# A reordered first normalisation, and casts bound behind a gelu, in a fused time-mix and GELU feed-forward kernel

## The chip, the cores and the metric

The kernel runs on one core of a Trainium2 chip. The metric is device time in microseconds (us) for one execution. A core has five engines with a queue each: TensorE (PE, with its weight loads PEld), VectorE (DVE), ScalarE (ACT), GpSimd (POOL) and SyncE (SP), which here issues all transfers between HBM and the on-chip memory. An engine works through its queue in order; semaphores tie the engines together.

## The reference

The input `x` has 4 sequences of 1024 tokens with 512 channels in float32. It is normalised per token to `xn`, and two branches are added to it.

```python
xn = _layernorm(x, axis=-1)
# branch 1, time mix: token t is mixed with token t-1 (token 0 with token 1)
xx = jnp.concatenate([xn[:, 1:2, :], xn[:, :-1, :]], axis=1) - xn
k = jnp.einsum('btc,hc->bth', xn + xx * time_mix_k, Wk)      # 704 hidden channels
r = jnp.einsum('btc,hc->bth', xn + xx * time_mix_r, Wr)
w = jnp.exp(-jnp.exp(time_decay))
state = state * w + jax.nn.relu(k_t)                        # a scan over t
out = layernorm(einsum(state * r_t, Wv)) * gamma + beta
# branch 2, feed-forward: 2048 hidden channels
X = xn.astype(jnp.float16)
D = jax.nn.gelu(jnp.dot(X.astype(jnp.float32), W0.T) + bias0, approximate=False).astype(jnp.float16)
E = jnp.dot(D.astype(jnp.float32), W1.T) + bias1
return x + out + E.astype(jnp.float16)
```

## The kernel before

The tokens are cut into 8 blocks of 512 (`blocks`), two for each sequence; a block has four tiles `s` of 128 tokens, and the 512 channels are four chunks `c` of 128. W0 and W1 are held as two parts, a rounded high part and the low rest (`split`, L123: ScalarE casts the high part, L124, VectorE subtracts it for the low part, L125), so that each product with them is made twice.

Each block goes through the same stages on TensorE:

- `attention` (L361): for each of six groups of hidden channels the products pk and pr (L385) from the mixed inputs `xk` and `xnT`; ScalarE takes the relu (L370), VectorE scans (L372) and multiplies by pr (L396).
- `ffn` (L470): `up(n)` (L475) makes the n-th of 16 hidden chunks, pd (L480), ScalarE takes its gelu to fp16 (L488), VectorE casts it to the product's type, d (L490). `down(n, s)` (L493) multiplies d with w1 and adds up pe (L495). Step n of the loop (L508) issues `up(n + 2)` and then the four `down(n, s)`. So a product up(n) has two further steps until down(n) wants its d.
- Between steps other work is issued, by the table `between` (L550): at step 0 `attention_out` (L413), at step 4 the next block's normalisation (`layernorm`, L189), at step 7 the next block's transposition on VectorE (`transposed`, L198, sixteen transposes at L204) and its mixing (`mixed_inputs`, L331). The mixing, for each chunk c, casts the normalised input to fp16 on ScalarE (L343), takes the difference to the token before (L348) and makes xk and then xnT from it (L350). xnT is overwritten in place, so its write has to wait for the cast that reads it.

Outside two stretches with an order written out by hand the framework's scheduler places the instructions in each engine's queue; the place at which work is issued in the program is its guide, not the final order.

Block 0 has extra work: W0 is loaded and split during `attention` (`load_w0`, L133), and W1 is loaded, split and written back to HBM in the split form during `ffn` (`load_w1`, L140; raw tiles from a ring of three, w1 tiles from another ring of three). Later blocks only read the split form back.

The first block's input has nothing to hide behind. `first_inputs` (L209) therefore has an order of its own under `manual_schedule` (L261 to L315). For each tile s: `stats` (L233) takes mean and variance on VectorE, `deviations` (L236) the square roots of two tiles on ScalarE, `inverses` (L241) their reciprocals on VectorE. `normalized` (L244) scales the tile: tile 0 on ScalarE with a shift computed on VectorE (L247, L248), the others on VectorE (L187). `turned` (L252) transposes the tile's four chunks on TensorE into `pts`. `busy(n)` (L228) issues n products of the identity with itself, whose result nobody reads; each appears as two instructions in the profile. Four edge transposes (L275) give the first two tokens, and a small one turns the mix rows (L284). Then ScalarE and VectorE build xk and xnT from the transposed chunks (L310, L313), and the first pk product can start. The fp16 casts of block 0 (L322) come after that.

Of the kernel before, what the change touches and what calls it, by code (L numbers as in the profile page):

```python
# [9 lines left out]
F32 = mybir.dt.float32  # L10
F32R = mybir.dt.float32r
AF = mybir.ActivationFunctionType
ALU = mybir.AluOpType

P = 128
# [4 lines left out]
def time_mix_and_gelu_ffn(  # L20
# [26 lines left out]
    nc = tc.nc  # L47
# [5 lines left out]
    NC = C // P  # L53
# [16 lines left out]
    const = pool("const", 1)  # L70
# [17 lines left out]
    ident = const.tile([P, P], F32, name="ident")  # L88
# [5 lines left out]
    eps_sb = const.tile([P, 1], F32, name="eps_sb")  # L94
    nc.vector.memset(eps_sb, EPS)
    mix_rows = const.tile([2 * NC, P], F32, name="mix_rows")
# [5 lines left out]
    b0_sb = const.tile([P, NN], F32, name="b0_sb")  # L102
# [106 lines left out]
    def first_inputs(xs, behind):  # L209

        pts = [ps_e.tile([P, TB], F32, tag="pe", name=f"pt_0_{c}") for c in range(NC)]
        idle = ps_mm.tile([P, TB], F32, tag="mm", name="idle")
        small = ps_mm.tile([P, TB], F32, tag="mm", name="small")
        tail = ps_mm.tile([P, TB], F32, tag="mm", name="tail")
        mix_t = small[:, : 2 * NC]
        late_t = tail[:, : NF + 1 + NN]
        edge = ps_mm.tile([P, TB], F32, tag="mm", name="edge")  # L220
        edge_t = edge[:, : NC * 2].rearrange("p (c t) -> p c t", t=2)
        mv = two.tile([P, NS, 2], F32, tag="mv", name="mvx_0")
        rstd = two.tile([P, NS], F32, tag=f"rstd{NS}", name="rx_0")
        shift0 = const.tile([P, 1], F32, name="shift0")
        ends = const.tile([P, NC, 2], F32, name="ends")
        xk = one.tile([P, NC, TB], F32, tag="xk", name="xk_0")

        def busy(n):  # L228

            for _ in range(n):  # L230
                nc.tensor.matmul(idle[:, :P], ident, ident, start=True, stop=True)

        def stats(s):  # L233
            stats_of(mv, s, xs[:, s, :], f"stx_0_{s}")

        def deviations(s0):  # L236
            nc.scalar.activation(
                rstd[:, s0 : s0 + 2], mv[:, s0 : s0 + 2, 1], AF.Sqrt, bias=eps_sb
            )

        def inverses(s0):  # L241
            nc.vector.reciprocal(rstd[:, s0 : s0 + 2], rstd[:, s0 : s0 + 2])

        def normalized(s):  # L244
            x_s, r = xs[:, s, :], rstd[:, s : s + 1]
            if s == 0:
                nc.vector.scalar_tensor_tensor(shift0, mv[:, 0, 0:1], -1.0, r, ALU.mult, ALU.mult)  # L247
                nc.scalar.activation(x_s, x_s, AF.Identity, bias=shift0, scale=r)  # L248
            else:
                normalize(x_s, x_s, mv[:, s, 0:1], r)  # L250

        def turned(s):  # L252
            for c in range(NC):
                nc.tensor.transpose(
                    pts[c][:, s * P : (s + 1) * P], xs[:, s, c * P : (c + 1) * P], ident
                )

        steps = [(0, 0), (1, 0), (0, 1), (1, 1), (2, 0), (3, 0), (2, 1), (3, 1)]  # L260
        with tc.manual_schedule(  # L261
            engines={nc.scalar.engine, nc.vector.engine, nc.tensor.engine}
        ):

            nc.scalar.activation(shift0, eps_sb, AF.Sqrt)
            busy(13)
            stats(0)
            stats(1)
            deviations(0)
            stats(2)  # L270
            inverses(0)
            normalized(0)
            turned(0)
            for c in range(NC):
                nc.tensor.transpose(  # L275
                    edge_t[:, c, :], xs[:2, 0, c * P : (c + 1) * P], ident[:2, :2]
                )
            busy(1)
            stats(3)
            deviations(2)  # L280
            normalized(1)
            nc.scalar.copy(ends, edge_t)
            turned(1)
            nc.tensor.transpose(mix_t, mix_rows, ident[: 2 * NC, : 2 * NC])  # L284
            nc.scalar.copy(mix_sb, mix_t)
            nc.scalar.activation(rest_sb, mix_t, AF.Identity, bias=1.0, scale=-1.0)
            inverses(2)
            normalized(2)
            turned(2)
            normalized(3)  # L290
            turned(3)
            nc.tensor.transpose(
                late_t, late_rows, ident[: NF + 1 + NN, : NF + 1 + NN]
            )
            busy(5)

            apart = two.tile([P, NC], F32, tag="apart", name="apart")
            nc.vector.tensor_sub(apart, ends[:, :, 1], ends[:, :, 0])
            for dst, m in ((xk[:, :, 0], mk_sb), (xnT[:, :, 1], mr_sb)):
                part = two.tile([P, NC], F32, tag="part", name="part")  # L300
                nc.vector.tensor_mul(part, apart, m)
                nc.vector.tensor_add(dst, part, ends[:, :, 0])
            for c, kind in steps:
                if kind == 0:
                    dst = part = xk[:, c, 1:]
                else:
                    ar = two.tile([P, TB], F32, tag="xx", name=f"ar_0_{c}")
                    dst, part = xnT[:, c, 2:], ar[:, 1:]
                j = kind * NC + c
                scaled = nc.scalar.activation(  # L310
                    part, pts[c][:, 1:], AF.Identity, scale=rest_sb[:, j : j + 1]
                )
                mixed = nc.vector.scalar_tensor_tensor(  # L313
                    dst, pts[c][:, : TB - 1], mix_sb[:, j : j + 1], part, ALU.mult, ALU.add
                )  # L315

        behind.enter_context(tc.issue_after(scaled.ins))
        behind.enter_context(tc.issue_after(mixed.ins))
        x16s = []
        for c, pt in enumerate(pts):  # L320
            x16 = four.tile([P, TB], F16, tag="x16", name=f"x16_0_{c}")
            nc.scalar.copy(x16, pt)  # L322
            x16s.append(x16)
            nc.scalar.copy(last[:, c, :], pt[:, TB - 1 :])

        nc.scalar.activation(w_sb, late_t[:, : NF + 1], AF.Exp)
        nc.scalar.activation(w_sb, w_sb, AF.Exp, scale=-1.0)
        nc.scalar.copy(b0_sb, late_t[:, NF + 1 :])
        return x16s, xk

    def mixed_inputs(i):  # L331

        t0 = blocks[i][1]
        if t0 > 0:
            nc.gpsimd.tensor_copy(xnT[:, :, 0:1], last)
        x16s = []
        xk = one.tile([P, NC, TB], F32, tag="xk", name=f"xk_{i}")
        for c in range(NC):
            now = xnT[:, c, 1:]
            if t0 == 0:  # L340
                nc.vector.tensor_copy(xnT[:, c, 0:1], now[:, 1:2])
            x16 = four.tile([P, TB], F16, tag="x16", name=f"x16_{i}_{c}")
            nc.scalar.copy(x16, now)  # L343
            x16s.append(x16)
            if t0 + TB < T:
                nc.gpsimd.tensor_copy(last[:, c, :], xnT[:, c, TB : TB + 1])
            xx = two.tile([P, TB], F32, tag="xx", name=f"xx_{i}_{c}")
            nc.vector.tensor_sub(xx, xnT[:, c, :TB], now)  # L348
            for dst, m in ((xk[:, c, :], mk_sb), (now, mr_sb)):
                nc.vector.scalar_tensor_tensor(  # L350
                    dst, xx, m[:, c : c + 1], now, ALU.mult, ALU.add
                )
        return x16s, xk
# [116 lines left out]
    def ffn(i, xf, between, state):  # L470
# [4 lines left out]
        def up(n):  # L475
            pd = ps_mm.tile([P, TB], F32, tag="mm", name=f"pd_{i}_{n}")
            cols = slice(n * P, (n + 1) * P)
            for c in range(NC):
                for w in (w0h, w0l):
                    nc.tensor.matmul(  # L480
                        pd,
                        w[c][:, cols],
                        xf[:, c, :],
                        start=(c == 0 and w is w0h),
                        stop=(c == NC - 1 and w is w0l),
                    )
            d16 = two.tile([P, TB], F16, tag="d16", name=f"d16_{i}_{n}")
            nc.scalar.activation(d16, pd, AF.Gelu, bias=b0_sb[:, n : n + 1])  # L488
            d = wide.tile([P, TB], F32R, tag="d", name=f"d_{i}_{n}", bufs=4)
            nc.vector.tensor_copy(d, d16)  # L490
            return d
# [36 lines left out]
    for i in range(len(blocks)):  # L528
# [16 lines left out]

        def next_inputs():
            transposed(x_now)
            state["mixed"] = mixed_inputs(i + 1)

        between = {0: out_stage}  # L550
        if more:
            between[4] = next_norm
            between[7] = next_inputs
        pe = ffn(i, xf, between, state)
        if more:
            x16s, xk = state["mixed"]
# [46 lines left out]
```

## Time and profile before

| | |
|---|---|
| Median of 4 runs | 944.82 us (944.48 to 945.03) |
| The profiled execution, its own time | 944.65 us |
| Its span, first to last instruction | 942.7 us |
| Start of the first pk product | 11.74 us |
| Busy share of TensorE / VectorE / ScalarE | 99% / 52% / 17% |
| Block 0, from its first pk to that of block 1 | 117.26 us |
| Blocks 1 to 6, each | 115.52 us |
| From the last block's first pk to the end | 120.41 us |

The profile is of one execution. A line of a timeline gives the start, the duration (of a whole run of instructions where they are merged), the engine, the line of the kernel, the operation, output and inputs, and in square brackets how long the engine sat idle before it and what ended that. A line of the waits gives who waited for whom, in total, how often, and the longest. The chain of waits follows the last instruction back to what released it, step by step; its dates cut the blocks above. Matmul ends are modelled, so neighbouring matmuls overlap in the listing; their starts are the better measure.

### The profile page before, as it was taken

To read this page: it belongs to the slowest core of one execution; us is meant where nothing else is said; L and a number is where in the kernel's file an instruction comes from. 1 tells how busy PE (TensorE), PEld (TensorE's weight loads), DVE (VectorE), ACT (ScalarE), POOL (GpSimd) and SP (SyncE) were. 2 spreads that over 40 slices of the span, in tenths; PEclk is the share of its full clock that TensorE was granted. 3 is DMA by queue.
4 is the path that set the end of the run, shared out by engine and by line. 5 is a ranking of instruction groups with operands and counts; after the bars stand their busy time and mean duration, and the time that the engine had idled before them with its cause. 6 is when DMAs were issued, how large, how long until landed. Compare 5 with 4: busy or idle time off the path is not lost.

```text
span 942.7 us, 8746 instructions
## 1 busy us (share of the span) xinstructions
PE 935.1 (99%) x3260; PEld 588.0 (62%) x3260; DVE 486.1 (52%) x842; ACT 162.7 (17%) x265; POOL 51.8 (5%) x124
## 2 busy tenths in 40 slices
PE   9999999999999999999999999999999999999998
PEld 6447764478544885448854588445884458744686
DVE  6558752484425944359343592426923279332513
ACT  6323410012100220102201021010210102111021
POOL 0010000100001000011000100002000020000100
PEclk9999999999999999999999999999999999999999
DMA  8734660035400454014530154302542023510243
GB/s 293 238 131 152 226 232 0 23 134 189 146 1 26 141 192 133 1 33 158 189 111 1 39 182 164 107 0 68 183 161 80 0 89 135 170 54 1 71 152 112
DMA packets 39573, 106.49 MB, mean 113 GB/s; under 512 B 4431, under 2 KB 4460, under 8 KB 39532
## 3 DMA queue, kind: packets, MB, share of 16 engines
q1 hardware_dynamic: 39532, 105.94, 33.3%
q8 instruction: 26, 0.43, 0.2%
q14 instruction: 15, 0.12, 0.0%
HBM read 89.14 MB, written 16.78 MB: 112 GB/s over the span
## 4 chain that ended last, share of the span: by engine, by line
PE 94%; DVE 4%; issue 1%; DMA 0%; ACT 0%; POOL 0%; SPq 0%; DVEq 0%
PE pd L480 23%; PE pe L495 22%; PE po L420 15%; PE pr L385 15%; PE pk L385 15%; PE pkr L385 3%; PE po L430 2%; DVE xnT L204 1%; DVE w L125 0%; DMA x<-in_L_attn_x 0%; DVE stx L183 0%; DVE d L490 0%; DVE z L467 0%; DVE e L466 0%; DVE xk L350 0%
## 5 line engine op out<-in xcount | busy, mean ns | idle before, releaser
L495 PE MATMUL pe<-w,d 128*128 128x512 f32 x1024 | 251.0, 389 | 1.4 <-DVE w L125 0.8
L495 PEld LDWEIGHTS pe<-w,d 128*128 128x128 f32 x1024 | 192.0, 188 | 42.3 <-DVE d L490 1.5
L480 PE MATMUL pd<-xf,w0h 128*128 128x512 f32 x512 | 203.5, 397 | 0.0
L480 PE MATMUL pd<-xf,w0l 128*128 128x512 f32 x512 | 199.4, 389 | 0.0
L488 ACT ACTIVATE d<-pd,b_sb 128x512 f16<-128x512 f32 x128 | 87.9, 687 | 418.8 <-PE pd L480 408.5
L385 PE MATMUL pr<-xnT,wr 128*128 128x512 f32 x320 | 144.2, 591 | 0.0
L385 PE MATMUL pk<-xk,wk 128*128 128x512 f32 x320 | 144.1, 592 | 0.0
L420 PE MATMUL po<-wv_sb,g 128*128 128x512 f32 x320 | 140.8, 595 | 0.0
L490 DVE CAST d<-d 128x512 fp32r<-128x512 f16 x128 | 54.0, 424 | 130.3 <-ACT d L488 129.3
L480 PEld LDWEIGHTS pd<-xf,w0h 128*128 128x128 f32 x512 | 96.1, 188 | 28.1 <-issue 5.7
L480 PEld LDWEIGHTS pd<-xf,w0l 128*128 128x128 f32 x512 | 96.1, 188 | 21.4 <-issue 1.9
L385 PEld LDWEIGHTS pr<-xnT,wr 128*128 128x128 f32 x320 | 60.5, 189 | 76.9 <-issue 75.7
L420 PEld LDWEIGHTS po<-wv_sb,g 128*128 128x128 f32 x320 | 60.1, 190 | 75.7 <-issue 75.0
L385 PEld LDWEIGHTS pk<-xk,wk 128*128 128x128 f32 x320 | 60.6, 190 | 73.4 <-issue 72.0
L204 DVE STREAM_TRANSPOSE xnT<-x 32x512 f32<-32x512 f32 x112 | 78.7, 703 | 2.2
L372 DVE TENSOR_TENSOR_SCAN st<-w_sb,carry,rk 128x512 f32<-128x512 f32 (+1 forms) x24 | 30.8, 1283 | 70.3 <-ACT rk L370 70.3
L370 ACT ACTIVATE rk<-pk 128x512 f32<-128x512 f32 x40 | 23.9, 597 | 233.6 <-PE pk L385 233.6
L183 DVE BATCH_NORM_STATS2 sty<-po 128x6 f32<-128x512 f32 x32 | 22.1, 689 | 73.5 <-PE po L430 67.9
L372 DVE TENSOR_TENSOR_SCAN st<-w_sb,rk 128x512 f32<-128x512 f32 (+1 forms) x24 | 29.3, 1222 | 55.3 <-ACT rk L370 53.5
L396 DVE TENSOR_TENSOR g<-st,pr 128x512 f32<-128x512 f32 x40 | 27.5, 687 | 53.6 <-PE pr L385 53.6
L177 POOL TENSOR_SCALAR ry<-mvy 128x1 f32<-128x1 f32 x32 | 11.4, 357 | 502.5 <-DVE mvy L184 502.5
L466 DVE TENSOR_TENSOR e<-pe,b_sb 128x512 f16<-128x512 f32 x32 | 20.8, 685 | 17.0 <-PE pe L495 17.0
(75 smaller groups left out, 458.7 us busy)
## 6 DMA issues: line engine op xcount, KB each, us to landing
w<-w1d SPq DMA_DIRECT2D x111, 512.0 KB, 3.2
x<-in_L_attn_x SPq DMA_DIRECT2D x32, 256.0 KB, 3.3
xres<-in_L_attn_x SPq DMA_DIRECT2D x32, 256.0 KB, 2.7
w1d<-w SPq DMA_DIRECT2D x16, 512.0 KB, 2.9
out<-z SPq DMA_DIRECT2D x32, 256.0 KB, 5.1
w0raw<-in_L_ffn_W SPq DMA_DIRECT2D x16, 256.0 KB, 4.9
w1raw<-in_L_ffn_W SPq DMA_DIRECT2D x16, 256.0 KB, 3.4
wk<-in_L_attn_Wk SPq DMA_DIRECT2D x4, 352.0 KB, 4.3
```

The source lines that it names most:

```text
L183: nc.vector.bn_stats(st6, src)
L204: nc.vector.transpose(dst[i * Q : (i + 1) * Q, :, :, j, :], src[j * Q : (j + 1) * Q, :, :, i, :],)
L370: nc.scalar.activation(rk[:hw], pk, AF.Relu)
L372: nc.vector.tensor_tensor_scan(st[:hw], w_sb[:hw, h : h + 1].to_broadcast([hw, TB]), rk[:hw], 0.0 if t0 == 0 else carry[:hw, h : h + 1], A ...
L385: nc.tensor.matmul(dst, w[c][:, cols], src, start=(c == 0), stop=(c == NC - 1))
L396: nc.vector.tensor_mul(g[:, h, :], st, pr)
L420: nc.tensor.matmul(pos[s], g[:, h, s * P : (s + 1) * P], wv_sb[:, h, :], start=(first and h == 0), stop=(not first and h == NF - 1),)
L466: nc.vector.tensor_add(e16, pe, b1_sb)
L480: nc.tensor.matmul(pd, w[c][:, cols], xf[:, c, :], start=(c == 0 and w is w0h), stop=(c == NC - 1 and w is w0l),)
L488: nc.scalar.activation(d16, pd, AF.Gelu, bias=b0_sb[:, n : n + 1])
L490: nc.vector.tensor_copy(d, d16)
L495: nc.tensor.matmul(pe[s], d[:, s * P : (s + 1) * P], w1[part], start=(n == 0 and part == 0), stop=(n == NN - 1 and part == 1),)
```

## The change

In the first block's order:

- tile 1 is normalised on ScalarE too, with a shift of its own (`shifts` has two columns);
- tile 2's statistics come after the reciprocals, shifts and scalings of tiles 0 and 1, directly ahead of tile 3's;
- on TensorE, the identity products at the start go from 13 to 11 calls, the one call between the edge transposes and tile 1 goes, and two calls stand behind the small transpose of the mix rows, ahead of tile 2. `turned(1)` and the small transpose are written before tile 3's statistics.

In the steady part:

- `mixed_inputs` takes the latest gelu that has been issued, and its four casts to fp16 are issued under `issue_after` that gelu, which holds them behind it in the scheduler's order;
- in block 0 the next block's transposition and mixing are issued at step 9 of the feed-forward loop instead of 7. The latest gelu is then that of up(10); in the other blocks it is that of up(8).

```diff
-        shift0 = const.tile([P, 1], F32, name="shift0")
+        shifts = const.tile([P, 2], F32, name="shifts")
...
-            if s == 0:
-                nc.vector.scalar_tensor_tensor(shift0, mv[:, 0, 0:1], -1.0, r, ALU.mult, ALU.mult)
-                nc.scalar.activation(x_s, x_s, AF.Identity, bias=shift0, scale=r)
+            if s < 2:
+                shift = shifts[:, s : s + 1]
+                nc.vector.scalar_tensor_tensor(
+                    shift, mv[:, s, 0:1], -1.0, r, ALU.mult, ALU.mult
+                )
+                nc.scalar.activation(x_s, x_s, AF.Identity, bias=shift, scale=r)
...
-            nc.scalar.activation(shift0, eps_sb, AF.Sqrt)
-            busy(13)
+            nc.scalar.activation(shifts[:, :1], eps_sb, AF.Sqrt)
+            busy(11)
             stats(0)
             stats(1)
             deviations(0)
-            stats(2)
             inverses(0)
             normalized(0)
+            normalized(1)
             turned(0)
             for c in range(NC):
                 nc.tensor.transpose(
                     edge_t[:, c, :], xs[:2, 0, c * P : (c + 1) * P], ident[:2, :2]
                 )
-            busy(1)
+            turned(1)
+            nc.tensor.transpose(mix_t, mix_rows, ident[: 2 * NC, : 2 * NC])
+            busy(2)
+            stats(2)
             stats(3)
             deviations(2)
-            normalized(1)
             nc.scalar.copy(ends, edge_t)
-            turned(1)
-            nc.tensor.transpose(mix_t, mix_rows, ident[: 2 * NC, : 2 * NC])
             nc.scalar.copy(mix_sb, mix_t)
...
-    def mixed_inputs(i):
+    def mixed_inputs(i, behind):
...
-            nc.scalar.copy(x16, now)
+            with tc.issue_after(behind.ins):
+                nc.scalar.copy(x16, now)
...
-            nc.scalar.activation(d16, pd, AF.Gelu, bias=b0_sb[:, n : n + 1])
+            state["gelu"] = nc.scalar.activation(d16, pd, AF.Gelu, bias=b0_sb[:, n : n + 1])
...
-            state["mixed"] = mixed_inputs(i + 1)
+            state["mixed"] = mixed_inputs(i + 1, state["gelu"])
...
-            between[7] = next_inputs
+            between[9 if i == 0 else 7] = next_inputs
```

## What I expect of the change

> **What bounds the kernel now.** I read the page's busy time by engine first (PE 99% of the span, DVE 52%), then the busy time by block, then TensorE's waits, then the timelines around the only gaps that these show. The blocks are cut at the first pk product of each (L385), as the chain of waits dates them.
>
> ```profile
> 11.91:129.17 117.26, 116.19 (x401) 72.39 (x401) 81.56 (x139) 44.09 (x77) 7.65 (x17) 1.00 0.61 212
> 129.17:244.69 115.52, 115.52 (x402) 72.41 (x401) 60.03 (x106) 16.55 (x26) 7.17 (x15) 1.00 0.31 103
> 244.69:360.21 115.52, 115.52 (x402) 72.41 (x401) 59.41 (x102) 16.55 (x26) 6.08 (x16) 1.00 0.30 101
> ```
>
> The columns are the stretch, its length, then busy time and count of PE, PEld, DVE, ACT and POOL. Blocks 1 to 6 are each 115.52 us long and TensorE is busy for all of it: nothing off TensorE can shorten them. Block 0 is 1.74 us longer. Before it lie 11.91 us in which the first block is normalised. So the change has two places in which to win: 1.74 us in block 0, and part of 11.91 us.
>
> TensorE's waits name the first place, and its timeline sizes it:
>
> ```profile
> PE pe L495 <- DVE w L125: 0.8, 1, 0.8
> PE pe L495 <- DVE d L490: 0.6, 2, 0.3
> ...
> 107.17 0.39 PE L480 MATMUL pd<-xf,w0l 128*128 128x512 f32 x1
> 107.87 0.50 PE L495 MATMUL pe<-w,d 128*128 128x512 f32 x1 [0.31 <-DVE d L490]
> 109.13 1.89 PE L495 MATMUL pe<-w,d 128*128 128x512 f32 x7 [0.76 <-DVE w L125]
> 110.86 0.39 PE L480 MATMUL pd<-xf,w0h 128*128 128x512 f32 x1
> ```
>
> Products follow each other every 0.227 us, so without a wait down(9) starts at 107.40 and the next up(12) 1.81 later, at 109.21. It starts at 110.86: 1.65 us lost. The rest of the 1.74 is 0.08 in the first pk products (11.91 to 13.71 where later fours take 1.72).
>
> Why VectorE is late there:
>
> ```profile
> 99.39 1.66 ACT L343 CAST x<-xnT 128x512 f16<-128x512 f32 x3 [3.87 <-DVE xnT L204]
> 100.96 0.68 ACT L488 ACTIVATE d<-pd,b_sb 128x512 f16<-128x512 f32 x1
> ...
> 107.39 0.42 DVE L490 CAST d<-d 128x512 fp32r<-128x512 f16 x1
> 107.72 0.75 DVE L350 SCALAR_TENSOR_TENSOR xnT<-xx,mix_sb,xnT 128x512 f32<-128x512 f32 x1
> 108.38 0.69 DVE L125 TENSOR_TENSOR w<-w1raw,w 128x512 fp32r<-128x512 f32 x1
> ```
>
> ScalarE stands 3.87 us before the casts of the next block's input, which wait for VectorE's transposes; gelu 8 is queued behind them, though its product ended at 96.52. VectorE then does the mixing for block 1 (L348, L350, 102.2 to 107.4) before d 9 and the low half of w1 9, which TensorE needs at 107.40. The mixing itself is not needed until 129.17.
>
> The second place, the opening:
>
> ```profile
> 5.35 0.69 DVE L183 BATCH_NORM_STATS2 stx<-x 128x6 f32<-128x512 f32 x1
> 5.44 0.29 ACT L237 ACTIVATE rx<-mvx,eps_sb 128x2 f32<-128x2 f32 x1 [3.23 <-DVE mvx L184]
> ...
> 6.17 0.13 DVE L242 RECIPROCAL rx<-rx 128x2 f32<-128x2 f32 x1
> 6.34 0.16 DVE L247 SCALAR_TENSOR_TENSOR shift<-mvx,rx 128x1 f32<-128x1 f32 x1
> ...
> 6.54 0.81 ACT L248 ACTIVATE x<-x,shift,rx 128x512 f32<-128x512 f32 x1 [0.80 <-DVE shift L247]
> ...
> 7.40 0.66 PE L254 MATMUL pt<-ident,x 128*128 128x128 f32 x4 [0.62 <-ACT x L248]
> ```
>
> The square root is done at 5.73, but the reciprocal waits behind the third tile's statistics until 6.17. From 7.40 on TensorE runs without a gap until the first product.
>
> **What the Trainium skill says.** "Perfetto Trace Analysis", Identifying the Most-Contended Engine, warns that matmul busy time overstates how close TensorE is to its limit. For blocks 1 to 6 the trace supports the bound otherwise: six equal lengths. "ScalarE: Activation LUTs", What ACT_TABLE_LOAD costs, gives 280 ns + 0.833 ns per element with a pointer bias, about 93 ns more for a pointer scale, and 93 ns of overlap between neighbours: an estimate of 0.80 us for a 512-wide tile, where the trace has 0.81; the second tile then follows 0.72 after the first. "TensorE: Matmul & The Clock Gate", What's actually happening, says that TensorE starts at half clock and needs a busy window of about 3.4 us. The trace agrees in kind: the idle products on the identity are 0.21 us apart until about 6.1 us and about 0.11 after it (the granted clock reads 1.00 throughout).
>
> **Opening, part by part.** The reciprocal moves ahead of the third tile's statistics. It can start at 5.73 + 0.04 = 5.77; the first shift follows 0.17 later (5.94), ScalarE 0.20 after that (6.14), and the first tile is normalised at 6.95: 0.40 us earlier, so the first transposes start at 7.00. The second shift is hidden beside ScalarE. The second tile goes to ScalarE at 6.14 + 0.72 = 6.86 and is done at 7.67; VectorE loses the 0.52 us operation for it. TensorE wants it after four transposes and the four edge transposes, at 7.00 + 0.93 = 7.93: covered by 0.26.
>
> What is late next is the rest of VectorE. Third statistics at about 6.10, fourth at 6.92 (before 6.42), its mean at 7.64; root on ScalarE at 7.86; reciprocal 8.18; third and fourth tiles at 8.39 and 8.87, done 8.91 and 9.41, 0.5 later than before. TensorE reaches the third at 9.06 to 9.26 and the fourth at 9.50 to 9.70: the cover is 0.1 to 0.2 us, and beyond it each delay counts in full.
>
> TensorE's own queue: the single idle call (two instructions) between edge and second tile goes, but two calls (four instructions) stand after the small transpose. Two more at 0.11 is 0.22 us to pay against 0.40 won. With each gap even at 0.11 the first transpose of the fourth tile, which starts ScalarE's first mix, comes at 9.55 against 9.83 (gain 0.28). With the 0.165 to 0.21 us that the trace shows behind an edge or small transpose, it comes at 9.61 to 9.70 (gain 0.13 to 0.22). Bounds: nothing, if the fourth tile is late; the whole 0.40 if the idle work costs nothing. I take 0.23. The eleven starting idle calls (two fewer, four instructions at 0.21) only follow the earlier transposes; the four small VectorE operations end at about 10.1, before the first mix at 10.7, so they stay hidden. The copy of the mix rows waits for nothing new. Everything behind (mix, idle, pk) is a fixed sequence and moves by the same 0.23. The weights' transfers are not moved in this stage.
>
> **Block 0.** The mixing moves from step 7 to step 9 and its casts are bound behind the latest gelu, number 10. As built, ScalarE does gelu 8, split 9, gelu 9, split 10, gelu 10, then the four casts. VectorE does the first two differences and xk products, d 8, then w 9, d 9, w 10, d 10, and only then the other mixing. I date them on the clock of before. Transposes still end at 99.36; gelu 8 starts at 96.7 instead of 100.96. VectorE: xx, w 8, xk, xx, d 8, xk to 102.87; w 9 to 103.5, d 9 to 103.9, needed at 107.40. Split 10 ends at 102.77, gelu 10 at 104.66, so w 10 and d 10 end at 105.1. The casts run 104.6 to 106.7 and the eight remaining mixing operations 105.2 to 110.4. d 11 ends at 110.8 and w 11 at 111.4, needed at 114.65. So the lost 1.65 us go, with at least 3.2 us of cover.
>
> SP's queue: the raw tiles 12 and 13 are requested behind w1 9 and 10 at about 104 and 105 (before: 111), between two loads of x; raw 14 and 15 stand behind the store of w1 13, at about 114.8 and 115.2. The longest landing that the trace shows for w1 here is 4.3 us, so 119.5; the halves then need ScalarE 0.62 and VectorE 0.69 each and are there by 121.6, needed at 123.72 and 125.53. In the first attention stage two loads of x change places with w0 loads; TensorE has no wait there and the last split of w0 on ScalarE ended at 46.6, before up(0) at 49.9. I cost these at nothing; with the cover gone, each late microsecond would be one on TensorE.
>
> **Blocks 1 to 6.** The casts now stand together behind gelu 8 instead of around gelu 7. In block 1 gelu 8 ends at about 214.6, the casts at about 216.8, gelu 9 at 218.2. VectorE has d 8 ahead of the first xnT product and does the same amount of work, so d 9 still ends at about 221.9; down(9) needs it at 224.75. The cover is 2.9 us. Cost nothing, and no gain either, since TensorE has no gap there.
>
> **Sum.** 1.65 + 0.23 = 1.88 us, taken as 1.9. The profiled execution took 944.65 (span 942.70 and 1.95 around it), so 942.75. The median of the runs is 944.82, 0.17 above it; against that, 942.9.
>
> **Rivals.**
> 1. The stall moves. VectorE's block of mixing, or raw 12 to 15 behind stores, holds a later down step of block 0. For: VectorE is busy without a pause from 100 to 110, and transfers took up to 4.3 us. Against: 3 us of cover at every step, 2.1 at the tightest. Half to all of 1.65 comes back: 943.7 to 944.6.
> 2. The opening gives nothing. The fourth tile is 0.3 us later than I count, or the clock stays at half through the next window, since idle products now end near 6.1 where it rises; some 17 transposes at 0.10 more are then 1.7 us. 943.2 to 944.7.
> 3. The whole lead of 0.40 reaches pk: 942.7.
> 4. Slower than before: gelu 9 and d 9 wait behind the casts in each of blocks 1 to 6. The work between d 8 and d 9 would have to end later than 224.75 by more than 1.9 / 6 = 0.32 us per block to undo the gain, and by 0.63 to be 0.2% slower than before: 946.8 then. Against: VectorE's sum does not grow and the cover is 2.9 us.
>
> **Numbers.** The 0.2% that a measurement of this kernel can tell from no change is 1.89 us, so the border stands at 942.93, inside my own forecast. Forecast 0.76, between 942.6 and 943.2, of which 0.40 lies below the border and 0.36 above; rival 1 0.06, rival 2 0.03, rival 3 0.12, rival 4 0.03. Faster 0.40 + 0.12 = 0.52; within 0.36 + 0.09 = 0.45; slower 0.03. The range takes in rival 3, the opening without gain (943.2) and half of the stall: 942.5 to 943.9.
>
> **What would show it.** Block 0 at 115.6 us with no wait of L495 on VectorE; first transposes at 7.0; first pk near 11.5 where it was 11.74; six blocks of 115.52. A block of 115.8 or more refutes the last part, a wait on d or w after 112 us the block 0 part, and a fourth tile that TensorE waits for, or transposes 0.21 apart, the opening.

## The result, and the profile after

| | before | after |
|---|---|---|
| Median of all executions | 944.82 us (51, from 944.47) | 942.68 us (31, from 942.43) |
| Ratio after / before | | 0.9977, 95% interval 0.9973 to 0.9982 |
| The profiled execution, its own time | 944.65 us | 942.97 us |
| First transposes | 7.40 us | 6.74 us |
| First pk product | 11.74 us | 11.30 us |
| First product of the narrow sixth group (pkr) in block 0 | 46.27 us | 46.15 us |
| The same in block 1 | 163.45 us | 161.77 us |
| Blocks 1 to 6, each | 115.52 us | 115.52 us |

The change is 2.14 us faster by the medians, beyond the 0.2% set as the border, though the interval reaches down to 0.18%. The forecast was 942.9. The two profiled executions differ by only 1.68, all of it gained by block 1's pkr product (163.45 − 161.77). That gap between 1.68 and 2.14 is the puzzle of this case: what follows block 0 is equally long in both, so it has to do with the opening, and a good part of the experiments is about it. One execution of run 9 below took 1203.53 us and is left out of its ratio.

Block 0 first. The view of the kernel after by stretches, with the columns used in the prediction; the cuts are again the first pk of each block:

```profile
11.46:127.09 115.63, 115.63 (x399) 71.90 (x399) 81.15 (x138) 44.20 (x77) 7.61 (x17) 1.00 0.63 217
127.09:242.61 115.52, 115.52 (x401) 72.41 (x400) 59.82 (x106) 16.65 (x26) 7.05 (x15) 1.00 0.30 103
```

Block 0 is 115.63 us long where it was 117.26, and TensorE is busy for all of it. TensorE's timeline at the former stall:

```profile
107.15 0.39 PE L485 MATMUL pd<-xf,w0l 128*128 128x512 f32 x1
107.37 1.98 PE L500 MATMUL pe<-w,d 128*128 128x512 f32 x8
109.19 0.39 PE L485 MATMUL pd<-xf,w0h 128*128 128x512 f32 x1
```

The eight products of down(9) are one unbroken run, and up(12) starts 1.82 after it. Before, that took 2.99 from a start already 0.47 late. ScalarE in the same stretch:

```profile
96.69 0.69 ACT L493 ACTIVATE d<-pd,b_sb 128x512 f16<-128x512 f32 x1 [1.19 <-PE pd L485]
...
103.95 0.69 ACT L493 ACTIVATE d<-pd,b_sb 128x512 f16<-128x512 f32 x1 [1.19 <-PE pd L485]
104.53 2.17 ACT L348 CAST x<-xnT 128x512 f16<-128x512 f32 x4
```

Gelu 8 starts when its product is there (96.69, before 100.96), and the four casts come in one piece behind gelu 10. VectorE:

```profile
102.83 0.68 DVE L125 TENSOR_TENSOR w<-w1raw,w 128x512 fp32r<-128x512 f32 x1
103.44 0.42 DVE L495 CAST d<-d 128x512 fp32r<-128x512 f16 x1
...
105.17 1.42 DVE L355 SCALAR_TENSOR_TENSOR xnT<-xx,mix_sb,xnT 128x512 f32<-128x512 f32 x2
```

w 9 and d 9 are done at 103.9, 3.5 us ahead of down(9); most of the mixing has moved behind them. Both queues have changed; runs 3, 4 and 10 will show that only VectorE's order matters.

The opening, in the timeline of the kernel after:

```profile
4.23 0.66 DVE L183 BATCH_NORM_STATS2 stx<-x 128x6 f32<-128x512 f32 x1
...
5.47 0.17 DVE L242 RECIPROCAL rx<-rx 128x2 f32<-128x2 f32 x1 [0.36 <-ACT rx L237]
5.67 0.23 DVE L248 SCALAR_TENSOR_TENSOR shifts<-mvx,rx 128x1 f32<-128x1 f32 x2
5.87 1.52 ACT L251 ACTIVATE x<-x,shifts,rx 128x512 f32<-128x512 f32 x2 [0.43 <-DVE shifts L248]
5.96 0.69 DVE L183 BATCH_NORM_STATS2 stx<-x 128x6 f32<-128x512 f32 x1
...
6.74 0.66 PE L257 MATMUL pt<-ident,x 128*128 128x128 f32 x4 [1.11 <-ACT x L251]
...
8.40 0.71 PE L231 MATMUL idle<-ident 128*128 128x128 f32 x4
...
8.95 1.04 PE L257 MATMUL pt<-ident,x 128*128 128x128 f32 x8
...
11.30 2.19 PE L390 MATMUL pk<-xk,wk 128*128 128x512 f32 x4
```

Two things here are not in the prediction. The tiles of x land at other times than in the profile of before, as they do from one execution to the next. There the second tile was late (statistics at 4.49, after 0.35 of waiting for x; here 4.23, without a wait) and the third early (landed by 5.34; here at 5.95, so that its statistics start 0.29 behind the first shift, where runs 1, 8, 9 and 10 have 0.14 or 0.15). And the first four pk products take 2.19 instead of 1.96: of the lead of 0.44 at pk (11.74 − 11.30), 0.12 is left at pkr.

Where it goes is seen in two places. The waits of SP's queue, kernel after:

```profile
SPq L117 <- DMA x<-in_L_attn_x: 1.2, 1, 1.2
```

And TensorE's weight loads in the timeline of the same kernel:

```profile
12.36 0.30 PEld L390 LDWEIGHTS pk<-xk,wk 128*128 128x128 f32 x2 [0.79 <-DVE xk L316]
```

The request for the first tile of wr stands 1.2 us in SP's queue until the third tile of x has landed (5.95), and the second tile of wk is requested behind it, at 6.65 where it was 5.99. The weight load blames xk, but xk's second chunk was done at 11.88 (10.47 and 1.41 for two): the only other input of that product is a tile of wk. That it is this one is inferred; the trace doesn't name it.

### The profile page after: what moved, and what is told of

Same layout as the page of the kernel before. It is cut to its first block, busy times and chain, and to the rows that moved or that the text cites. A ratio compares the mean times of both kernels' runs of the same rounds, so it can differ in the third digit from the quotient of the medians.

```text
span 941.0 us, 8756 instructions
## 1 busy us (share of the span) xinstructions
PE 934.0 (99%) x3258; PEld 586.9 (62%) x3258; DVE 484.6 (51%) x842; ACT 164.0 (17%) x266; POOL 51.4 (5%) x124
## 4 chain that ended last, share of the span: by engine, by line
PE 98%; DVE 1%; DMA 0%; ACT 0%; issue 0%
PE pd L485 25%; PE pe L500 24%; PE po L425 15%; PE pk L390 15%; PE pr L390 15%; PE pkr L390 3%; PE po L435 2%; DVE z L472 0%; DMA x<-in_L_attn_x 0%; DVE e L471 0%; PE pt L257 0%; PE idle L231 0%; DVE stx L183 0%; ACT x L251 0%; ACT d L493 0%
```

## The experiments

Medians stand beside the median of the kernel before on the same chip. Runs 1 to 4 shared one chip, 5 to 8 another, 9 to 12 a third.

| Run | Median, us | Before, us | Ratio, 95% interval |
|---|---|---|---|
| 1 opening alone | 944.18 | 945.03 | 0.9992 (0.9984 to 1.0000) |
| 2 steady part alone | 943.08 | 945.03 | 0.9980 (0.9973 to 0.9987) |
| 3 binding alone | 944.95 | 945.03 | 1.0001 (0.9993 to 1.0009) |
| 4 step 9 alone | 943.24 | 945.03 | 0.9984 (0.9977 to 0.9990) |
| 5 third statistics back | 943.57 | 944.80 | 0.9998 (0.9989 to 1.0007) |
| 6 second tile on VectorE | 942.68 | 944.80 | 0.9979 (0.9971 to 0.9988) |
| 7 late rows behind weights | 943.65 | 944.80 | 0.9989 (0.9981 to 0.9997) |
| 8 the change once more | 942.64 | 944.80 | 0.9977 (0.9968 to 0.9985) |
| 9 no idle calls at the small transpose | 942.51 | 944.83 | 0.9979 (0.9970 to 0.9988) |
| 10 no binding | 942.81 | 944.83 | 0.9981 (0.9975 to 0.9988) |
| 11 three parts out | 942.74 | 944.83 | 0.9981 (0.9974 to 0.9987) |
| 12 wk ahead of wr | 943.10 | 944.68 | 0.9982 (0.9976 to 0.9989) |

The ratios lie close to the quotients of the means, so they need not equal those of the medians: the two groups of executions of run 5 pull its ratio to 0.9998. The table below is read from TensorE's and VectorE's timelines, one profiled execution each: the start of the third tile's statistics, of the first transposes, of pk, of block 0's pkr, of the first product of the output stage (po), and the time from block 0's pkr to block 1's. Runs 2 to 4 have the old opening; run 5 has the old place of the statistics. The profiled executions of runs 2, 4, 5 and 7 took 946.45, 945.03, 945.30 and 945.96 us, more than 1.7 above the medians of their runs: their rows show what can happen, not what usually does.

| Kernel | stats 3 | transposes | pk | pkr | po | pkr to pkr |
|---|---|---|---|---|---|---|
| before | 5.35 | 7.40 | 11.74 | 46.27 | 53.64 | 117.18 |
| 2 steady | 5.98 | 8.04 | 15.38 | 49.82 | 57.18 | 115.51 |
| 3 binding | 5.95 | 8.01 | 12.35 | 46.88 | 54.25 | 117.15 |
| 4 step 9 | 6.00 | 8.06 | 13.96 | 48.41 | 55.76 | 115.50 |
| 5 stats back | 5.95 | 8.01 | 14.14 | 48.59 | 55.94 | 115.50 |
| after | 5.96 | 6.74 | 11.30 | 46.15 | 53.49 | 115.62 |
| 1 opening | 5.67 | 6.59 | 11.17 | 45.70 | 53.05 | 117.14 |
| 6 tile 2 DVE | 6.18 | 6.71 | 11.47 | 46.00 | 53.37 | 115.52 |
| 7 late rows | 5.83 | 6.75 | 13.70 | 49.24 | 56.61 | 115.52 |
| 8 after again | 5.72 | 6.64 | 11.48 | 46.01 | 53.36 | 115.50 |
| 9 no idle | 5.69 | 6.61 | 10.98 | 45.73 | 53.34 | 115.88 |
| 10 no binding | 5.69 | 6.61 | 11.17 | 45.70 | 53.05 | 115.50 |
| 11 three out | 6.01 | 6.53 | 11.29 | 45.82 | 53.17 | 115.53 |
| 12 wk first | 5.70 | 6.62 | 10.99 | 46.14 | 53.93 | 116.07 |

**Runs 1 to 4: the change taken apart.** Run 1 has the new opening, no binding, and the mixing at step 7 everywhere:

```diff
-            with tc.issue_after(behind.ins):
-                nc.scalar.copy(x16, now)
+            nc.scalar.copy(x16, now)
...
-            between[9 if i == 0 else 7] = next_inputs
+            between[7] = next_inputs
```

> Only the opening is changed (reciprocal ahead, tile 1 on ScalarE, TensorE's small work moved); block 0's mixing stays at step 7 without a binding. Theory A (the opening was mis-sized: 0.23 us forecast, about 0.45 real, since the median of all runs fell by 2.14 and block 0 explains 1.65): 944.3 to 944.4, ratio 0.9995, and the stall of down(9) is still there with 1.5 to 1.7 us. Rival B (the opening gives nothing because the next thing, the weights' transfers or g, takes the lead back, as in the profiled execution after the change, where only 0.02 of 0.44 us was left at 100 us): 944.8, ratio 1.000.

Run 2 has the reverse: the opening of before, with the binding and step 9.

```diff
-            nc.scalar.copy(x16, now)
+            with tc.issue_after(behind.ins):
+                nc.scalar.copy(x16, now)
...
-            between[7] = next_inputs
+            between[9 if i == 0 else 7] = next_inputs
```

> Only the steady part is changed (casts bound behind the gelu, block 0's mixing at step 9); the opening is that of before. Theory A: 944.82 less 1.65 is 943.2, ratio 0.9983, no wait of TensorE on d or w1 in block 0. Rival B (all of the gain comes from here): 942.7, ratio 0.9977.

Run 3 is before with the binding alone:

```diff
-            nc.scalar.copy(x16, now)
+            with tc.issue_after(behind.ins):
+                nc.scalar.copy(x16, now)
```

> Only the binding: casts issued behind the latest gelu in every block, block 0's mixing still at step 7. The built order of block 0 is then that of before, and in blocks 1 to 6 TensorE has no gap to give. Theory A: no change, 944.8, ratio 1.000, stall of 1.65 us in block 0 as before, six blocks of 115.52. Rival (the binding is what removes the stall): 943.2. Rival (the binding costs in blocks 1 to 6): 945 or more, blocks of over 115.6.

Run 4 is before with step 9 alone:

```diff
-            between[7] = next_inputs
+            between[9 if i == 0 else 7] = next_inputs
```

> Only block 0's mixing moved from step 7 to 9, casts unbound, opening of before. Built, VectorE has w1 9 and d 9 among the mixing instead of behind it, while ScalarE still has the casts ahead of gelu 8. Theory A (the step alone removes the stall, the binding is idle): 943.2, ratio 0.9983, no wait on d or w1. Rival (the binding is needed, since gelu 8 and 9 still queue behind the casts that wait for the transposes): a wait of 0.3 to 1.5 us at down(8) or down(9) stays, 943.5 to 944.8.

Measured: run 1 is 0.85 faster than its before (the interval of its ratio just touches 1), run 2 1.95, run 3 0.08, run 4 1.79. With the binding alone both waits of before are still there, in TensorE's waits of run 3:

```profile
PE pe L496 <- DVE w L125: 0.8, 1, 0.8
PE pe L496 <- DVE d L491: 0.6, 2, 0.3
```

They are there although gelu 8 no longer stands behind the casts. ScalarE's and VectorE's timelines of run 3, whose block 0 runs 0.6 us later than that of before:

```profile
97.32 0.69 ACT L489 ACTIVATE d<-pd,b_sb 128x512 f16<-128x512 f32 x1 [1.19 <-PE pd L481]
99.99 2.19 ACT L344 CAST x<-xnT 128x512 f16<-128x512 f32 x4 [1.98 <-DVE xnT L204]
...
107.98 0.42 DVE L491 CAST d<-d 128x512 fp32r<-128x512 f16 x1
108.97 0.69 DVE L125 TENSOR_TENSOR w<-w1raw,w 128x512 fp32r<-128x512 f32 x1
```

Gelu 8 starts as soon as its product is there, and yet d 9 and w 9 stand behind the mixing on VectorE as before. With step 9 alone the waits are gone. The view by stretches of run 4, for 115.5 us from 46.5 us on, has TensorE busy for all of them:

```profile
46.50:162.00 115.50, 115.50 (x401) 72.43 (x400) 72.48 (x122) 28.92 (x46) 5.34 (x12) 1.00 0.45 156
```

In the last column of the table all kernels at step 7 have 117.14 to 117.18, and all at step 9, bound or not, 115.50 to 115.62 (115.88 and 116.07 in runs 9 and 12, where the output stage waits). So the 1.65 us of block 0 are step 9's, shown in both directions; the binding has no part in them. At step 7 it changes ScalarE's order in block 0 but not VectorE's; the expectation, that nothing in block 0's order would change, was wrong for ScalarE.

Runs 1 and 2 together give 2.80, more than the change's 2.14 and 2.16 (run 8). The interval of run 1's ratio alone is 0.76 us either way, so the parts add up within what these runs can tell.

**Run 5: the third tile's statistics back in their old place**, all else as after.

```diff
             deviations(0)
+            stats(2)
             inverses(0)
...
             busy(2)
-            stats(2)
             stats(3)
```

> The changed kernel with one thing undone: the third tile's statistics stand ahead of the first reciprocal again. Theory A (the reciprocal used to wait for the landing of the third tile, 5.95 us in most executions, and not only for 0.4 us of VectorE's work): first statistics of tile 2 to first transpose 2.05 us as before, so transposes at 8.0 where tile 2 lands at 5.95, the first pk near 12.4, and a time 0.5 to 1.0 us above the changed kernel, 943.3 to 943.8, with more executions near 945 to 947 where TensorE's clock falls back in the longer pause. Rival B (only VectorE's 0.4 us): transposes about 0.4 later, 942.9 to 943.1.

Seven executions took 942.87 to 943.57, six took 945.03 to 946.62; the profiled one is of the later six (945.30). Its timeline:

```profile
5.95 0.69 DVE L183 BATCH_NORM_STATS2 stx<-x 128x6 f32<-128x512 f32 x1 [0.87 <-DMA x<-in_L_attn_x]
...
6.78 0.13 DVE L242 RECIPROCAL rx<-rx 128x2 f32<-128x2 f32 x1
...
8.01 0.66 PE L257 MATMUL pt<-ident,x 128*128 128x128 f32 x4 [1.84 <-ACT x L251]
...
9.98 1.22 PE L231 MATMUL idle<-ident 128*128 128x128 f32 x4
...
10.99 1.83 PE L257 MATMUL pt<-ident,x 128*128 128x128 f32 x8
```

and the same stretch in the view by stretches, where the third number from the right is the granted TensorE clock:

```profile
9.00:12.00 3.00, 3.00 (x15) 2.65 (x15) 1.69 (x8) 0.41 (x3) 0.00 (x0) 0.53 0.97 300
```

VectorE stands 0.87 us before the statistics until the third tile of x has landed. The reciprocal of the first two tiles, whose square root has long been ready (5.12 + 0.29), stands behind them. The first transposes come at 8.01 instead of 6.74. TensorE has by then been idle for 1.84 us, and from 9 to 12 us its clock is 0.53: the eight transposes of the last two tiles take 1.83 instead of 1.04, and the first pk starts 2.84 later than after.

The column "stats 3" shows the rule. With the statistics first, the transposes start 2.05 or 2.06 after them, in before and in runs 2 to 5. With the reciprocal first they start at 6.53 to 6.75, whether the third tile lands early or, as in after, at 5.95. Counted from the first tile's statistics, whose own start differs by 0.2 us, they come 3.33 to 3.35 later in every kernel with the reciprocal first, but 4.17 later in before and 4.61 to 4.72 in runs 2 to 5. This is what the move does: it takes the third tile's landing off the path. The profile of before did not show it, because there the third tile had landed before VectorE was free (5.35).

**Run 6: the second tile on VectorE**, as before the change.

```diff
-            if s < 2:
+            if s == 0:
```

> The changed kernel with tile 1 normalised on VectorE, right behind tile 0's shift. Theory A (VectorE's chain to tile 3 is what TensorE reaches last): tiles 2 and 3 are 0.45 us later, the first transpose of tile 3 moves by 0.3 to 0.4, first pk at about 11.75: 943.0 to 943.1 against 942.7 for the changed kernel. Rival (idle work on TensorE still covers it): no difference, 942.7.

942.68, against 942.64 of the change itself beside it. VectorE gets to the third statistics later (6.18) and the last two tiles reach TensorE 0.1 to 0.2 us later in its profile, but that cannot be seen in the time. Scaling the second tile on ScalarE is worth nothing that these runs can tell.

**Run 7: the loads of the late rows behind the second pair of weights**, so that SP reaches the weights sooner.

```diff
-    nc.sync.dma_start(late_rows[:NF], rows(decay[:H0]))
-    nc.sync.dma_start(late_rows[NF : NF + 1, :HF], decay[H0:].rearrange("(c p) -> c p", p=HF))
-    nc.sync.dma_start(late_rows[NF + 1 :], rows(bias0))
...
         nc.sync.dma_start(wr_sb[c], wrT[c * P : (c + 1) * P, :])
+        if c == 1:
+            nc.sync.dma_start(late_rows[:NF], rows(decay[:H0]))
...
```

> The changed kernel with the three small late_rows transfers moved behind the first two pairs of wk and wr, so that the second wk is not held in SP's queue by tile 2's landing. Theory A (in the changed kernel the weights' landing holds the second and fourth pk product, 0.31 us in its profiled execution): pk four-groups of 1.80 and 1.72 instead of 2.03 and 1.81, 942.3 to 942.5. Rival (the late rows come too late for their transpose, or the weights delay tiles 2 and 3): 942.7 to 943.5, and TensorE waits at L295 or at a tile's transposes.

943.65: 1.0 slower than the change beside it. The rival holds. TensorE's timeline of run 7, then its view by stretches:

```profile
8.96 1.04 PE L260 MATMUL pt<-ident,x 128*128 128x128 f32 x8
11.77 0.21 PE L298 MATMUL tail<-ident,late_rows 22*128 22x22 f32 x1 [1.78 <-DMA late_rows<-in_L_ffn_bias]
...
12.00:15.00 3.00, 3.00 (x12) 2.38 (x13) 2.90 (x5) 2.68 (x5) 0.00 (x0) 0.58 0.93 311
```

The transpose of the late rows stands ahead of the pk products in TensorE's order and waits 1.78 us: three small rows queued behind four 352 KB tiles of weights are as late as these. This execution took 945.96, by far the slowest of run 7: behind the wait TensorE's clock falls to 0.58. How long the usual executions wait isn't shown; that the wait makes up their 1.0 us is inferred.

**Run 8: the change once more**, on the chip of runs 5 to 7, no edit.

> The changed kernel itself, beside the three others on one chip and for a second profile of its opening: 942.7. Theory A says first transposes 6.6 to 6.8 whatever the landing of tile 2, first pk 11.3 to 11.5.

942.64. Its profile shows the same opening with the third tile landing early (wr requested at 5.58): no wait for wk, pk in 1.96. But its first transposes are slow. TensorE's timeline of run 8:

```profile
6.64 0.93 PE L257 MATMUL pt<-ident,x 128*128 128x128 f32 x4 [0.23 <-ACT x L251]
7.50 0.41 PE L278 MATMUL edge<-ident,x 2*128 2x2 f32 x4
```

and the same place in run 10:

```profile
6.61 0.65 PE L257 MATMUL pt<-ident,x 128*128 128x128 f32 x4 [0.39 <-ACT x L251]
7.19 0.41 PE L278 MATMUL edge<-ident,x 2*128 2x2 f32 x4
```

0.86 to the next operation against 0.58: four transposes still at the slow pace of the start, 0.28 us. So the same queue gives pk at 11.48 or at 11.17.

**Run 9: without the two idle calls behind the small transpose.**

```diff
             nc.tensor.transpose(mix_t, mix_rows, ident[: 2 * NC, : 2 * NC])
-            busy(2)
             stats(2)
```

> The kernel after without the two idle calls (four small instructions of TensorE) that stand behind the small transpose. Theory (the idle instructions hold TensorE: the third tile is normalised at about 8.9, and its transposes start only at about 9.5): the transposes of the third tile start 0.2 to 0.4 us earlier and the lead reaches the store, 942.2 to 942.4. Rival (the lead is taken back behind it: by the fourth tile on VectorE, by the landing of the second weight tile at about 12, or by a TensorE clock that falls in the gap left): first pk product as before or the later ones waiting for the weights, 942.6 or more; with the clock at half in 9 to 12 us 944 or more.

942.51: the best median here, but its interval overlaps that of the change, and the theory's 942.2 to 942.4 was not reached. From the first transposes to pk it takes 4.37 (10.98 − 6.61), where the change takes 4.56 (11.30 − 6.74) and before 4.34. So two more idle calls on TensorE cost about what the prediction charged, 0.22 by after against before. Taking both out gives 0.19, since TensorE then waits 0.22 us for the third tile. TensorE's timeline of run 9:

```profile
10.98 2.07 PE L389 MATMUL pk<-xk,wk 128*128 128x512 f32 x4
...
14.61 1.99 PE L389 MATMUL pk<-xk,wk 128*128 128x512 f32 x4
...
53.34 1.13 PE L424 MATMUL po<-wv_sb,g 128*128 128x512 f32 x2
```

The pk products stand apart for their weights again, and po starts at 53.34, only 0.02 ahead of run 8 (53.36), although pk started 0.50 ahead of it. From pkr on another 0.38 is lost (115.88), 0.26 of it ahead of po: pkr to po takes 7.61 instead of 7.35. Run 12 shows what stands there.

**Runs 10 and 11.** Run 10 is the change without the binding:

```diff
-            with tc.issue_after(behind.ins):
-                nc.scalar.copy(x16, now)
+            nc.scalar.copy(x16, now)
```

> The kernel after without the binding of the four casts behind a gelu; step 9 in block 0 stays. Theory (the binding does nothing for the time: in block 0 step 9 alone removes the stall, in blocks 1 to 6 TensorE has no wait with or without it): 942.65, as the kernel after, block 0 at 115.6 us and blocks 1 to 6 at 115.52. Rival (at step 9 the unbound casts hold a gelu or a split again): a wait on d or w in block 0 of 0.3 us or more, 943.0 or more.

The view by stretches of run 10, from pkr to pkr in block 0, and ScalarE's and VectorE's timelines ahead of its down(9), which starts at 106.81:

```profile
45.70:161.20 115.50, 115.50 (x401) 72.43 (x400) 72.02 (x121) 28.58 (x45) 5.72 (x12) 1.00 0.45 155
...
98.79 1.66 ACT L347 CAST x<-xnT 128x512 f16<-128x512 f32 x3 [3.86 <-DVE xnT L204]
100.36 0.68 ACT L492 ACTIVATE d<-pd,b_sb 128x512 f16<-128x512 f32 x1
...
102.93 0.69 DVE L125 TENSOR_TENSOR w<-w1raw,w 128x512 fp32r<-128x512 f32 x1
104.79 0.42 DVE L494 CAST d<-d 128x512 fp32r<-128x512 f16 x1
```

No wait of TensorE without the binding, and block 0 is as long as with it. ScalarE still stands 3.86 us ahead of the casts, and gelu 8 still comes behind three of them. But VectorE has w 9 and d 9 done at 103.6 and 105.2, in the middle of the mixing: 1.6 us ahead of down(9), where the binding leaves 3.5. With run 3 this settles the cause. ScalarE's late gelu 8 did no harm; VectorE's order alone made the stall, and step 9 changes that order. The median is 942.81 against 942.64 and 942.68; intervals overlap, and nothing in the trace stands behind the difference. Run 11 takes out the binding, the second tile's place on ScalarE and the two idle calls:

```diff
-            if s < 2:
+            if s == 0:
...
-            busy(2)
...
-            with tc.issue_after(behind.ins):
-                nc.scalar.copy(x16, now)
+            nc.scalar.copy(x16, now)
```

> The kernel after with what earlier runs found idle taken out: no binding, the second tile normalised on VectorE as in the kernel before, and no idle calls behind the small transpose. Left are the statistics behind the first reciprocal, the earlier order of TensorE and step 9. Theory (only these act): the same as without the idle calls alone, 942.2 to 942.4. Rival (the parts need each other: the second tile on VectorE puts the statistics of the third and fourth tile 0.5 us later, and without the idle instructions TensorE waits for them): a wait for the third or fourth tile of 0.3 us or more, 942.6 or more.

942.74, within the change's interval. In its profile TensorE waits 0.37 for the third tile, in the place of the idle instructions: the rival's mechanism, at a price of nothing, since those would have filled it. The theory's 942.2 to 942.4 was not reached. What is left after all this, the reciprocal ahead of the third statistics, TensorE's earlier order and step 9, carries all of the gain that these runs can tell.

**Run 12: wk ahead of wr**, on top of run 9.

```diff
     for c in range(NC):
         nc.sync.dma_start(wk_sb[c], wkT[c * P : (c + 1) * P, :])
+    for c in range(NC):
         nc.sync.dma_start(wr_sb[c], wrT[c * P : (c + 1) * P, :])
```

> The run without the two idle calls, with the four loads of wk ahead of the four of wr; no other engine's order changes. There the first products of pk stood apart for their weights (2.07 and 1.99 us for four instead of 1.80 and 1.72), and wr is needed only 1.8 us later. Theory (the lead of the opening is taken back by wk landing behind wr in SP's queue): the fours of pk at 1.96 and 1.88 us as recorded without a wait, the remainders of pk and pr 0.2 us earlier, 942.3. Rival (the transfers as a whole bound the opening: the wait goes to wr, or to the splits of w0 ahead of the first product of the output stage): pr or the output stage gives back as much, 942.5 as without the new order, or more.

943.10, about 0.6 above run 9 by the medians; the ratios differ by only 0.0003, within their intervals. The theory's 942.3 was missed in any case. TensorE's timeline of run 12:

```profile
10.99 1.97 PE L390 MATMUL pk<-xk,wk 128*128 128x512 f32 x4
13.31 1.99 PE L390 MATMUL pr<-xnT,wr 128*128 128x512 f32 x4 [0.36 <-DMA wr<-in_L_attn_Wr]
...
53.93 8.85 PE L425 MATMUL po<-wv_sb,g 128*128 128x512 f32 x20 [0.28 <-DVE g L401]
```

The pk products now have their weights, and the wait goes to pr, which waits 0.36 for wr. pkr is 0.41 later than in run 9, and po waits 0.28 for g. Some pieces of the chain of waits of run 12 ahead of po, each with its start, length and what ran, then two lines of ScalarE's timeline:

```profile
42.40 3.46 DMA w0raw<-in_L_ffn_W
...
47.25 2.94 DMA w1raw<-in_L_ffn_W
...
53.20 0.69 DVE g L401
...
50.22 0.62 ACT L125 CAST w<-w1raw 128x512 fp32r<-128x512 f32 x1 [0.81 <-DMA w1raw<-in_L_ffn_W]
50.74 0.59 ACT L375 ACTIVATE rk<-pk 128x512 f32<-128x512 f32 x1
```

The chain runs through the transfers of the raw tiles of W0 and of the first of W1. The relu of the fifth group stands in ScalarE's queue behind their splits. Its pk products were issued by 42.6 (pr's start then), but it runs at 50.74, after ScalarE has stood 0.81 us for a tile of W1, and the scan and g follow it. Run 9 has the same order and the same wait (relu at 50.08). So the rival holds for these two profiles: with pk at 11 us the wait goes to a transfer behind, not to the normalisation. But it is a wait in ScalarE's queue as much as one for a transfer: whether a relu ahead of the splits, or more than three buffers for the raw tiles, would free g was not tried. No faster version than the change was shown.

## Why the prediction was right, and where its sizes were off

**Block 0: right in place and size, 1.65 us.** 117.18 became 115.62 from pkr to pkr, and 115.50 in run 8, where the output stage did not wait; without step 9 it is 117.14 to 117.18, so the stall is 1.64 to 1.68. w 9 and d 9 were forecast to end at 103.9 and ended there; the casts were forecast for 104.6 to 106.7 and ran from 104.53. "With at least 3.2 us of cover" held: no wait for d or w is left after 107 us except one of 0.3 that the last block has in every kernel. The reason was half right. Credit was given to the pair "The mixing moves from step 7 to step 9 and its casts are bound", and "gelu 8 is queued behind them" was counted among the causes. Step 9 alone removes the stall with gelu 8 as late as before (100.36 in run 10), and an early gelu 8 without it removes nothing (97.32 in run 3): the cause is the mixing ahead of w 9 and d 9 on VectorE. One reading was short: "The longest landing that the trace shows for w1 here is 4.3 us", but the two w1 loads that before requests at 96.4 and 101.1 took 4.7. The cover of 2.1 us was then 1.7, and nothing came of it.

**Opening: the mechanism right, its size off.** The step was the 0.40 us by which the first transposes move ahead ("so the first transposes start at 7.00"). They moved by 0.65 to 0.87, to 6.53 to 6.75. The term came from one execution of before, in which the second tile was late (statistics at 4.49, in all other profiles 4.03 to 4.25) and the third early. I read the reciprocal's wait as the duration of the third statistics; in runs 2 to 5 it was above all the wait for the third tile of x. "I take 0.23" became about 0.5 by difference (2.14 − 1.65 by the medians), and 0.85 in run 1, the opening alone. That the forecast total came within 0.2 us is in part luck: the transposes gained more than was counted, and part of that was lost again further on. The Trainium skill says this of VectorE's queue, in "DVE: scalar operands, raw-bit mode, write accounting and state across instructions", Flops that outlive an instruction: it is one in-order queue. The 0.87 us in run 5 are what that costs when the instruction at its head waits for a transfer.

**The idle instructions: right in size.** "Two more at 0.11 is 0.22 us to pay": 4.56 against 4.34. In the time of a whole execution they can't be seen (run 9).

**"I cost these at nothing": half wrong.** The transfers were called not moved in this stage, but work that moves ahead of fixed transfers meets them. In the profile of after, 0.32 of the lead of 0.44 was lost between pk and pkr, 0.23 of it in the first four products, and 0.12 more in block 0 (115.62 against 115.50), where a weight load of the output stage waits 0.3 us for g. That makes up the profiled pair: 0.12 + 1.68 − 0.12 = 1.68. That pair compares an early third tile with a late one. With like beside like the opening gives more: early, before against runs 8 and 10 has pkr 0.26 and 0.57 ahead; late, run 3 against after 0.73. The 0.5 by difference lies between.

**Blocks 1 to 6: right.** 115.52 in all kernels, but for one of 115.58 in run 3.

**The rivals.** Rival 1, the stall moves, fell: no new wait in block 0. Rival 3 named 942.7, which was measured, but not for its reason: the idle work had its price, and the lead was larger. Rival 2's slow clock exists, on the other side: it can strike the old opening when the third tile is late (runs 2, 4 and 5, not run 3), and in the profiles of the new one it shows only as 0.28 and 0.24 us at the first transposes (runs 8 and 11). Run 7's slow stretch comes from its own wait. Rival 4 fell with the blocks of 115.52.

**Open.** The request of wr 0, which waits for the third tile's landing, stands at 5.34 in before, at 5.95 to 6.00 in runs 2 to 5, at 5.95 in after and at 5.41 to 5.58 in runs 1, 6, 8, 9, 10 and 11. Why it takes one of two times, and whether the kernel has a part in it, was not tried. How many ordinary executions of before have it late can't be read from their times, so the 0.5 is not divided further. Two parts of the change were never taken out alone: the shorter run of identity products at the start, and the earlier place of the second tile's transposes.

## What to carry to other kernels

An instruction that nothing waits for is not harmless at the head of an in-order queue: if its input comes by a transfer, put it behind the work that is ready, and look at several executions before sizing the gain, since one profile shows one landing. When a stall goes, look for the move that removes it alone; here one changed step number gave three quarters of the gain, and the binding beside it gave nothing that these runs can tell. When two engines' queues change at once, a run with each change alone tells which order mattered; the profile of the pair does not. Once the computation of an opening is ahead of its loads, shortening it further or swapping loads may only move the wait, as it did in runs 9 and 12.

## What the runs showed of the hardware

Gaps of 1.50 us (run 4), 1.84 (run 5) and 1.95 (run 2) on TensorE were each followed by a granted clock of 0.50 to 0.53 in the stretch from 9 to 12 us, and one of 1.78 (run 7) by 0.58 from 12 to 15 us, while gaps of 0.62 (before) and 0.88 (run 3) and one of 1.11 (after) left it at 1.00. The Trainium skill, "TensorE: Matmul & The Clock Gate", HAM oscillation, gives the abstract rule that no gap on TensorE should pass about 3.4 us. Here about half of that was enough, soon after the start; the measurement decides. In runs 2 to 5 the gap ends at 8.01 to 8.06 and is as long as it is because the identity products of the start end anywhere from 6.09 (run 2) to 7.13 (run 3). Whether the length of the gap decides, or the share of work in the time before it, these runs don't separate.

The fall does not always come at once. In runs 4 and 5 the first four transposes after the gap still run fast (0.58 and 0.59 to the next operation) and the following ones slow, so the price falls on work that did not wait. In run 2 the four were slow already (1.02), and in run 7 the ten identity products behind the gap took 2.00 instead of 1.38.
